# A two-layer graph network: the weighted sum is put inside the second list's branch, and the second FFN's rest is put beside the second attention

## The chip, the cores and the metric

The kernel runs on one core of one Trainium2 chip, in one launch. The metric is the device time of that launch in microseconds. The core has five engines with their own instruction queues, each worked off in order: PE (TensorE, matmuls), DVE (VectorE), ACT (ScalarE), POOL (GpSimd, here the issuer of gathers) and SP (SyncE, the issuer of most other transfers). ACT issues some transfers too. A transfer issued by any of them is carried by the same 16 DMA engines.

## What is computed

`x` is 6250 rows of 256. There are two layers; each is a graph step and then an FFN with a choice of experts, every one on layer-normed rows and added to `x`:

```python
# layer 0, graph: attention over 206250 sorted edges, 4 heads of 64
e = leaky_relu(a_src[src] + a_dst[dst]); p = exp(e - segment_max(e, dst)[dst])
out = relu(segment_sum(p / denom[dst] * h[src], dst) + bias)
# layer 0, FFN: 8 experts, the best 2 of each row, hidden width 1024
out = sum over the 2 of weight * (gelu(ln(x) @ W1[e] + b1[e]) @ W2[e] + b2[e])
# layer 1, graph: a weighted sum over the same 206250 edges
nb = segment_sum(edge_val[:, None] * emb[edge_src], edge_dst)
o = leaky_relu(emb @ W1.T + b1 + (nb + nb * emb) @ W2.T + b2);  out = o / norm(o)
# layer 1, FFN: 4 experts of width 512; the gates come from an attention
# over 131072 other, unsorted edges and a loop at each node (4 heads of 4)
g = gates(gat(x @ W_gat, edge_index)); out = sum_e g_e * (gelu(x @ W1[e]) @ W2[e])
```

## The kernel before

All matrices are float32. The rows of `x` stay in SBUF as `X`, 49 blocks of 128 rows. Edges are taken in tiles of 128, and 8 tiles (`Q`) make a piece. A gather fetches 128 table rows by an index column; POOL issues one for each tile (L1214 in the attentions, L234 in the weighted sum).

The work is staged in time, as the trace shows it:

1. Checks of the first edge list, then the first attention (`gat_stream` with `s0`), to 2245 us.
2. The first FFN (`ffn0`, `routed_ffn`): 56 tiles of 256 sorted rows, 2475 to 3342 us. Each tile has 32 matmuls of L601, four transposes of L586, 32 matmuls of L614. Beside it runs a generator: `sorted_edges` sorts the second edge list (172 steps), then `runs_of` turns the first list into the tables of the weighted sum (indices `si_d`, weights `wab_d`, places `dab_d`), in two chunks of rows. After each FFN tile the code takes four steps, "for _ in range(4): next(beside, None)". A step ends at a `yield`. This part is not ordered by hand: the program order gives priorities to a scheduler, which fills the engines' queues when the kernel is built.
3. The FFN's result is fetched (`yy`, seven loads) and added to `X` (L632).
4. The weighted sum (`fast`, from L1885): `X` is layer-normed (L256) into the table `tab_ef`; then for each piece 8 gathers, the sums of runs on ACT (L1920) and DVE (L1922), one-hot matmuls that place the sums (L2011), and once a block of rows is whole, a chain of functions `side`, `dense`, `norm`, `next_ln`, `next_h`, one link a step. `next_h` writes the row of the second attention's table `tab_1f` (L1986) and the same with one part more into `ha_d` (L1987). When four blocks are done, `start(g)` puts the second FFN's work for them on a list.
5. The second FFN (`dense_ffn`) computes all 4 experts for every row: `inner` is four matmuls (L1654) and a gelu on ACT (L1659), `outer` eight matmuls (L1665), a copy on ACT (L1670) and a write to `y_d` (L1671). A call of `beside()` takes one piece of work off the list. The weighted sum calls it three times per step, and after its last step calls it until the list is empty.
6. A flag, found while sorting, says whether the second list may be taken the fast way: `tc.If(v1 == 1)`. Inside, `layer1_fast` loads `si1s`, `HN`, `dl1s` and `il1s`, prepares the node values and runs `gat_stream` with `s1` (99 pieces). Its own `beside` is called five times per piece and adds the gated results of the FFN, read from `y_d`, to `X` (L1756).

In stages 1, 4, 5 and 6 the order of the main loops is written out by hand ("with tc.manual_schedule()"): each engine gets its instructions in the order of the code. The lines that set the pace of stage 6 are

```python
g = piece[q] = mp.tile([P, Q, W], F32, name="g", bufs=9)      # L1212: freed after messages(q)
...
beside()                                                       # five times in each step
```

Instructions inside a branch are not mixed with instructions outside it. Memory for tiles comes from pools; a pool opened where an earlier one lay waits until the earlier one's tiles are done with.

Of the kernel before, what the change touches and what calls it, by code (L numbers as in the profile page):

```python
# [32 lines left out]
P = 128  # L33
LN_EPS = 1e-5
BIG = float(2**100)
CH = 7
# [35 lines left out]
def tile_kernel(ctx, tc, src_ins, out):  # L72
# [1447 lines left out]
    def runs_of(s, sp, pp, si, wab, dab):  # L1520
# [19 lines left out]
        def turned(dst, src):  # L1540
            d, t = (a.rearrange("p (r j) -> p r j", j=Q) for a in (dst, src))
            for j0 in range(0, Q, 4):
                pt = pp.tile([P, 4, P], F32, name="pt_s")
                for j in range(4):
                    nc.tensor.transpose(pt[:, j], t[:, :, j0 + j], ident)
                nc.scalar.copy(d[:, :, j0:j0 + 4].rearrange("p r j -> p j r"), pt)

        for c in range(-(-npiece // P)):
# [4 lines left out]
            nc.vector.tensor_copy(b, a.bitcast(I32))  # L1553
            nc.vector.tensor_scalar(x, b, 0.0, float(N), op0=OP.is_lt, op1=OP.mult)
            nc.vector.tensor_add(b, b, x)
            nc.vector.tensor_scalar(b, b, 0.0, float(N - 1), op0=OP.max, op1=OP.min)
            yield
            y = room("B1")
            turned(y, b)
# [10 lines left out]
            turned(d, b)  # L1570
            yield
            load(w, I["edge_weight"], c, nr)
            wt = room("A0")
            turned(wt, w)
            yield
            d3 = d.rearrange("p (r j) -> p r j", j=Q)
            first = d3[:, :, 0:1].to_broadcast([P, P, Q])
            for k, op in enumerate((OP.is_equal, OP.not_equal)):
                m = room(("A1", "B1")[k])
                nc.vector.tensor_tensor(m.rearrange("p (r j) -> p r j", j=Q), d3, first, op=op)  # L1580
                nc.vector.tensor_mul(m, m, wt)
# [103 lines left out]
    def layer1_fast(s1, si1, dl1, il1, ha_d, tab_1, y_d):  # L1685
# [3 lines left out]
        with tc.tile_pool(name="g1f", bufs=1) as g1, tc.tile_pool(name="f1w", bufs=2) as fp:  # L1689
            si = g1.tile([P, s1.C * P], I32, name="si1s")  # L1690
            nc.sync.dma_start(si, si1)
            HN = g1.tile([P, NT, W1 + H1], F32, name="HN")
            nc.sync.dma_start(HN, ha_d)
# [75 lines left out]
            def beside():  # L1769
                if work:  # L1770
                    work.pop(0)()
                return bool(work)
# [5 lines left out]
    def fast(flag_s0, last_d, dl_d):  # L1778
# [104 lines left out]
        ha_d = dram.tile([P, NT, D1 + 2 * H1], F32, name="ha_d")  # L1883
        y_d = dram.tile([NT, P, C1, D], F32, name="y_d")
        with tc.tile_pool(name="n1e", bufs=2) as mp:  # L1885
            for t0, n in chunks(NT, CH):
                em = mp.tile([P, CH, D], F32, name="em")
                layernorm(mp, em, X[:, t0:t0 + n, :], n)
                nc.sync.dma_start(tab_e[t0 * P:(t0 + n) * P].rearrange("(t p) d -> p t d", p=P), em[:, :n])
        with tc.tile_pool(name="n1f", bufs=1) as ep, tc.tile_pool(name="n1fw", bufs=2) as mp, \  # L1890
                tc.tile_pool(name="n1f_ps", bufs=1, space=PSUM) as pp, \
                tc.tile_pool(name="f1_ps", bufs=2, space=PSUM) as fpp:
            si = ep.tile([P, npiece * Q], I32, name="si8")
            nc.sync.dma_start(si, si_d)
            wab = ep.tile([P, 2, npiece * Q], F32, name="wab")
            nc.sync.dma_start(wab, wab_d.rearrange("k p t -> p k t"))
            dab = ep.tile([P, npiece * 2], F32, name="dab")
            nc.sync.dma_start(dab, dab_d)
            w12 = ep.tile([P, 2, KD, D], F32, name="w12")
            nc.sync.dma_start(w12[:, 0], I["L1_gnn_W1"].rearrange("(k p) f -> p k f", p=P))  # L1900
            nc.sync.dma_start(w12[:, 1], I["L1_gnn_W2"].rearrange("(k p) f -> p k f", p=P))
            bb = ep.tile([P, 2, D], F32, name="bb12")
            nc.sync.dma_start(bb[:, 0], rows(I["L1_gnn_b1"]))
            nc.sync.dma_start(bb[:, 1], rows(I["L1_gnn_b2"]))
            bias = ep.tile([P, D], F32, name="bias12")
            nc.vector.tensor_add(bias, bb[:, 0], bb[:, 1])
            wg = layer1_weights(ep)
            room, start, beside = dense_ffn(ep, mp, fpp, y_d)
            ips = place_iota(pp)
            acc, piece, runs, ems, sums_of = {}, {}, {}, {}, {}  # L1910

            def sum_runs(q):

                g = piece.pop(q)
                r = [mp.tile([P, D], F32, name=f"run{i}", bufs=3) for i in range(2)]
                for j in range(Q):
                    for i in range(min(2, j + 1)):
                        w = wab[:, i, q * Q + j:q * Q + j + 1]
                        if j == i:
                            nc.scalar.activation(r[i], g[:, j, :], AF.Copy, scale=w)  # L1920
                        else:
                            nc.vector.scalar_tensor_tensor(r[i], g[:, j, :], w, r[i], op0=OP.mult, op1=OP.add)  # L1922
                oh = mp.tile([P, 2, P], F32, name="oh", bufs=3)
                nc.vector.tensor_tensor(oh, ips[:, None, :P].to_broadcast([P, 2, P]),  # L1924
                                        dab[:, 2 * q:2 * q + 2, None].to_broadcast([P, 2, P]), op=OP.is_equal)
                runs[q] = r, oh

            def move(i, kept):

                whole = []  # L1930
                for b in range(NT):
                    of = s0.parts_of(b)
                    if i in of:
                        if b not in sums_of:
                            sums_of[b] = pp.tile([P, D], F32, name="bacc1", bufs=2)
                            ems[b] = mp.tile([P, D], F32, name="emb", bufs=3)
                            nc.sync.dma_start(ems[b], tab_e[b * P:(b + 1) * P])
                        nc.tensor.matmul(sums_of[b], shift_to(s0, i, b), kept, start=(i == of[0]), stop=(i == of[-1]))
                        if i == of[-1]:
                            whole.append(b)  # L1940
                return whole

            def side(b):
                sd = mp.tile([P, D], F32, name="sd_", bufs=2)
                nc.vector.scalar_tensor_tensor(sd, ems[b], 1.0, sums_of.pop(b), op0=OP.add, op1=OP.mult)
                eT = mp.tile([P, KD, P], F32, name="eT")
                transposed(pp, eT, ems.pop(b))
                sT = mp.tile([P, KD, P], F32, name="sT")
                transposed(pp, sT, sd)
                return eT, sT  # L1950

            def dense(b, eT, sT):
                po = pp.tile([P, KD, P], F32, name="pt").rearrange("p k e -> p (k e)")
                for k in range(KD):
                    nc.tensor.matmul(po, eT[:, k], w12[:, 0, k], start=(k == 0), stop=False)
                for k in range(KD):
                    nc.tensor.matmul(po, sT[:, k], w12[:, 1, k], start=False, stop=(k == KD - 1))
                o = mp.tile([P, D], F32, name="on")
                nc.vector.tensor_add(o, po, bias)
                nc.vector.scalar_tensor_tensor(o, o, 0.2, o, op0=OP.mult, op1=OP.max)  # L1960
                return o

            def norm(b, o):
                sq = mp.tile([P, D], F32, name="sq", bufs=1)
                ss = mp.tile([P, 1], F32, name="ss")
                nc.scalar.activation(sq, o, AF.Square, accum_out=ss)
                nc.scalar.activation(ss, ss, AF.Sqrt)
                nc.vector.tensor_scalar_max(ss, ss, 1e-12)
                nc.vector.reciprocal(ss, ss)
                nc.vector.scalar_tensor_tensor(X[:, b, :], o, ss, X[:, b, :], op0=OP.mult, op1=OP.add)  # L1970

            def next_ln(b):
                xl = mp.tile([P, 1, D], F32, name="xl1")
                layernorm(mp, xl, X[:, b:b + 1, :], 1)
                return xl

            def next_h(b, xl):
                o = b % GB * P
                xT = room(b // GB)[:, :, o:o + P]
                transposed(pp, xT, xl[:, 0, :])  # L1980
                ph = pp.tile([P, KD, P], F32, name="pt")[:, 0, :D1 + 2 * H1]
                for k in range(KD):
                    nc.tensor.matmul(ph, xT[:, k], wg[:, k], start=(k == 0), stop=(k == KD - 1))
                h = mp.tile([P, D1 + 2 * H1], F32, name="h1")
                nc.vector.tensor_copy(h, ph)
                nc.sync.dma_start(tab_1[b * P:(b + 1) * P], h[:, :D1 + H1])  # L1986
                nc.sync.dma_start(ha_d[:, b, :], h)  # L1987
                if b % GB == GB - 1 or b == NT - 1:
                    start(b // GB)

            chain = {side: dense, dense: norm, norm: next_ln, next_ln: next_h}


            with tc.manual_schedule():
# [88 lines left out]
```

## Time and profile before

| what | value |
|---|---|
| median of 3 runs | 6830.59 us (6827.94 to 6841.34) |
| the profiled execution | 6821.2 us |
| its span, first to last instruction | 6819.3 us |
| instructions | 61938 |
| busy: PE, DVE, ACT, POOL | 58%, 59%, 17%, 62% of the span |
| granted TensorE clock, mean | 0.746 of full speed |
| moved by DMA | 822.99 MB, mean 121 GB/s |

How to read what follows. A line of the timeline gives start, length, engine, code line, instruction, the tile written and the tiles read, their shapes, how many instructions are merged, and in brackets how long the engine had been idle and what released it. "SPq" and "ACTq" are instructions with which SP and ACT issue a transfer. A line of a table by stage gives the window, its length, then busy time and number of instructions of each engine, the granted TensorE clock, the busy share of the DMA engines and the GB/s. "issue" as a releaser means that nothing in the profile held the engine.

### The profile page before, as it was taken

How to read it: one execution, taken by the hardware profiler on the slowest of the kernel's cores; microseconds unless marked ns; L12 is line 12 of the kernel's file. 1: busy time of each engine (PE TensorE's matmuls, PEld its weight loads, DVE VectorE, ACT ScalarE, POOL GpSimd, SP SyncE). 2: the span in 40 equal slices, each digit the busy share in tenths (PEclk: the TensorE clock that was granted, in tenths of full speed). 3: DMA queues.
4: the chain of work that ended last, by engine and by line, in shares of the span. 5: the costliest groups of instructions: out<-in, count | busy, mean ns of one | idle time of the engine just before them, and what ended most of it. 6: DMA issues, size and time to landing. Idle time of an engine off the chain costs nothing.

```text
span 6819.3 us, 61938 instructions
## 1 busy us (share of the span) xinstructions
PE 3924.9 (58%) x17463; PEld 2934.8 (43%) x17463; DVE 4025.0 (59%) x9984; ACT 1166.6 (17%) x2834; POOL 4252.7 (62%) x4320
## 2 busy tenths in 40 slices
PE   4466665666666579998624566666666665111111
PEld 3344444444444468886513444444444443111111
DVE  5455555555555872443356565555566651788888
ACT  2000000000000112232112233323333332000000
POOL 0777777777777012332167777777777772777774
PEclk9677777777777589998856787778787887555555
DMA  4545555545554145556543444444444441223222
GB/s 135 139 137 139 138 138 139 138 138 138 138 137 128 45 128 194 186 185 206 163 152 105 110 115 113 112 112 113 112 114 114 113 113 53 64 66 66 68 66 56
DMA packets 502756, 822.99 MB, mean 121 GB/s; under 512 B 149744, under 2 KB 321987, under 8 KB 502370
## 3 DMA queue, kind: packets, MB, share of 16 engines
q0 software_dynamic: 190880, 462.26, 25.6%
q1 hardware_dynamic: 298854, 345.00, 16.5%
q10 hardware_dynamic: 12668, 11.68, 0.6%
q8 instruction: 141, 2.31, 0.1%
q14 instruction: 213, 1.74, 0.1%
HBM read 743.88 MB, written 77.89 MB: 121 GB/s over the span
## 4 chain that ended last, share of the span: by engine, by line
PE 26%; DVE 22%; POOL 19%; issue 15%; DMA 13%; ACT 4%; DVEq 0%; SPq 0%; another core or an unknown queue 0%; POOLq 0%; ACTq 0%
POOL g L1214 15%; DVE run L1922 7%; DMA g<-tab,si 7%; PE ph L601 5%; PE py L614 4%; POOL g L234 4%; PE acc L2011 4%; PE acc L1316 3%; PE pf L1654 2%; DMA g<-tab_1f,si1s 2%; DVE X L1756 2%; PE pf L1665 2%; DMA g<-tab_ef,si 2%; DVE g L1293 1%; PE pt L263 1%
## 5 line engine op out<-in xcount | busy, mean ns | idle before, releaser
L234 POOL DMA_INDIRECT g<-tab_ef,si x1616 | 1688.6, 1045 | 591.0 <-issue 437.0
L1214 POOL DMA_INDIRECT g<-tab,si x1612 | 1540.8, 956 | 494.3 <-issue 408.9
L1316 PE MATMUL acc<-g,oh 128*128 128x264 f32 x3224 | 1042.5, 488 | 338.8 <-DVE g L1293 333.9
L1922 DVE SCALAR_TENSOR_TENSOR run<-g,wab,run 128x256 f32<-128x256 f32 x2626 | 1088.8, 478 | 98.9 <-DMA g<-tab_ef,si 65.7
L1316 PEld LDWEIGHTS acc<-g,oh 128*128 128x128 f32 x3224 | 772.0, 247 | 560.4 <-DVE g L1293 394.5
L1214 POOL DMA_INDIRECT g<-tab_1f,si1s x787 | 770.1, 979 | 247.8 <-issue 213.3
L2011 PE MATMUL acc<-run,oh 128*128 128x256 f32 x808 | 336.9, 559 | 857.5 <-DVE oh L1924 857.2
L2011 PEld LDWEIGHTS acc<-run,oh 128*128 128x128 f32 x808 | 195.0, 265 | 993.4 <-DVE oh L1924 834.6
L1246 DVE TENSOR_TENSOR z<-g,nd 128x32 f32<-128x32 f32 (+1 forms) x301 | 57.7, 192 | 752.3 <-DMA g<-tab,si 654.2
L1293 DVE TENSOR_TENSOR g<-g,pe 128x2048 f32<-128x2048 f32 (+2 forms) x301 | 486.8, 1617 | 0.0
L1316 PE MATMUL acc<-s,oh 128*128 128x72 bf16 x1267 | 96.7, 251 | 601.4 <-DVE s L1298 601.4
L1654 PE MATMUL pf<-xt,w 128*128 128x512 f32 (+1 forms) x832 | 424.6, 650 | 1.5 <-ACT h L1659 1.0
L1665 PE MATMUL pf<-w,h 128*128 128x256 f32 x1568 | 413.9, 417 | 12.6 <-ACT h L1659 12.6
L601 PE MATMUL ph<-xe,w 128*128 128x256 f32 x1792 | 404.7, 382 | 0.0
L614 PE MATMUL py<-w,h 128*128 128x256 f32 x1792 | 400.7, 381 | 0.0
L577 POOL DMA_INDIRECT xg<-tab_x,gi x112 | 123.2, 1100 | 408.1 <-PE pt L586 322.4
L1665 PEld LDWEIGHTS pf<-w,h 128*128 128x128 f32 x1568 | 333.7, 214 | 86.8 <-ACT h L1659 17.5
L601 PEld LDWEIGHTS ph<-xe,w 128*128 128x128 f32 x1792 | 341.3, 192 | 45.6
L614 PEld LDWEIGHTS py<-w,h 128*128 128x128 f32 x1792 | 337.2, 191 | 43.3
L1316 PEld LDWEIGHTS <-oh 128*128 128x128 bf16 x1267 | 90.2, 134 | 605.2 <-issue 500.8
L1235 PEld LDWEIGHTS <-ot 128*128 128x128 bf16 x2879 | 116.1, 102 | 457.7 <-DVE ot L1224 403.3
L617 POOL DMA_INDIRECT tab_y<-y,so x112 | 118.6, 1059 | 296.6 <-DVE y L616 292.4
(486 smaller groups left out, 5689.4 us busy)
## 6 DMA issues: line engine op xcount, KB each, us to landing
w<-in_L_ffn_W SPq DMA_DIRECT2D x112, 1024.0 KB
db<-s_d SPq DMA_DIRECT2D x299, 256.0 KB
g<-tab_ef,si POOLq DMA_INDIRECT x1616
g<-tab,si POOLq DMA_INDIRECT x1612
y_d<-y SPq DMA_DIRECT2D x196, 128.0 KB
yb<-y_d SPq DMA_DIRECT2D x49, 512.0 KB
g<-tab_1f,si1s POOLq DMA_INDIRECT x787
yy<-tab_y SPq DMA_DIRECT2D x7, 1792.0 KB
```

Of the source, the lines that this page charges most:

```text
L234: nc.gpsimd.indirect_dma_start(out=dst, out_offset=None, in_=table, in_offset=bass.IndirectOffsetOnAxis(ap=si[:, t:t + 1], axis=0))
L577: nc.gpsimd.indirect_dma_start(out=xg[:, i, :], out_offset=None, in_=tab_x, in_offset=bass.IndirectOffsetOnAxis(ap=gi[:, 2 * j + i:2 * j + ...
L601: nc.tensor.matmul(ph, w1[:, k, f * P:(f + 1) * P], xe[:, k, :], start=(k == 0), stop=(k == KD - 1))
L614: nc.tensor.matmul(py, hs[f][:, i * P:(i + 1) * P], w2[:, f, :], start=(f == 0), stop=(f == FC - 1))
L1214: nc.gpsimd.indirect_dma_start(out=g[:, j, :DH + H], out_offset=None, in_=tab, in_offset=bass.IndirectOffsetOnAxis(ap=si[:, t0 + j:t0 + j ...
L1293: nc.vector.tensor_mul(gh, gh, ps[i][:, o:o + n, :, None].to_broadcast([P, n, H, CD]))
L1316: nc.tensor.matmul(acc[b].rearrange("p s w -> p (s w)"), oh[:, t - a], m_, start=(t == lo), stop=(t == hi))
L1654: nc.tensor.matmul(ph[:, :n], w1[:, e, k, f * P:(f + 1) * P], xts[g][:, k, :n], start=(k == 0), stop=(k == KD - 1))
L1665: nc.tensor.matmul(py[:, :D], hs[g, e, f][:, j * P:(j + 1) * P], w2[:, e, f, :], start=(f == 0), stop=(f == FC - 1))
L1756: nc.vector.scalar_tensor_tensor(X[:, b, :], v[:, e, :], gates[:, j, e:e + 1], X[:, b, :], op0=OP.mult, op1=OP.add)
L1922: nc.vector.scalar_tensor_tensor(r[i], g[:, j, :], w, r[i], op0=OP.mult, op1=OP.add)
L2011: nc.tensor.matmul(acc[i], oh[:, k], r[k], start=(q % 2 == 0 and k == 0), stop=(last and k == 1))
```

## The change

Three things are changed.

- The weighted sum becomes a function, `weighted_sum(room, start, beside, HN)`, with the layer norm that fills `tab_ef` at its head. A new function `with_ffn(then)` opens pools for the second FFN, `HN` and `si1s`, calls `dense_ffn`, the weighted sum and then `then`. The flag is read and the branch entered before all this; the weighted sum is traced once in each arm.
- `next_h` writes its result into `HN` in SBUF, and `tab_1f` from there. `ha_d` is gone. The weighted sum no longer empties the FFN's list at its end. The second attention's `beside` first takes FFN work, and adds gated results only when none is left. In the other arm `finish` empties the list first.
- In `runs_of` a chunk has 17 steps where it had 8: each `turned` yields after each of its two halves, and a few vector operations get a step of their own. `run` has 2 buffers for 3, `kept1` 2 for 3; the FFN's tiles come from a pool of their own (`f1o`).

```diff
 # runs_of
                 nc.scalar.copy(d[:, :, j0:j0 + 4].rearrange("p r j -> p j r"), pt)
+                yield
...
             nc.vector.tensor_copy(b, a.bitcast(I32))
+            yield
             nc.vector.tensor_scalar(x, b, 0.0, float(N), op0=OP.is_lt, op1=OP.mult)
+            yield
             nc.vector.tensor_add(b, b, x)
+            yield
...
-            turned(y, b)
+            yield from turned(y, b)
...
-            turned(d, b)
-            yield
+            yield from turned(d, b)
             load(w, I["edge_weight"], c, nr)
             wt = room("A0")
-            turned(wt, w)
-            yield
+            yield from turned(wt, w)
...
                 nc.vector.tensor_tensor(m.rearrange("p (r j) -> p r j", j=Q), d3, first, op=op)
+                yield
                 nc.vector.tensor_mul(m, m, wt)
 # layer1_fast
-    def layer1_fast(s1, si1, dl1, il1, ha_d, tab_1, y_d):
+    def layer1_fast(s1, si, dl1, il1, HN, tab_1, y_d, rest):
-            si = g1.tile([P, s1.C * P], I32, name="si1s")
-            nc.sync.dma_start(si, si1)
-            HN = g1.tile([P, NT, W1 + H1], F32, name="HN")
-            nc.sync.dma_start(HN, ha_d)
...
             def beside():
-                if work:
+                if not rest() and work:
                     work.pop(0)()
                 return bool(work)
 # fast
-        ha_d = dram.tile([P, NT, D1 + 2 * H1], F32, name="ha_d")
+        def weighted_sum(room, start, beside, HN):
...
-                r = [mp.tile([P, D], F32, name=f"run{i}", bufs=3) for i in range(2)]
+                    r = [mp.tile([P, D], F32, name=f"run{i}", bufs=2) for i in range(2)]
...
-                h = mp.tile([P, D1 + 2 * H1], F32, name="h1")
-                nc.vector.tensor_copy(h, ph)
-                nc.sync.dma_start(tab_1[b * P:(b + 1) * P], h[:, :D1 + H1])
-                nc.sync.dma_start(ha_d[:, b, :], h)
+                    nc.vector.tensor_copy(HN[:, b, :], ph)
+                    nc.sync.dma_start(tab_1[b * P:(b + 1) * P], HN[:, b, :D1 + H1])
...
-                while beside():
-                    pass
+        def with_ffn(then):
+            with tc.tile_pool(name="f1e", bufs=1) as ep, tc.tile_pool(name="f1o", bufs=2) as fp, \
+                    tc.tile_pool(name="f1_ps", bufs=2, space=PSUM) as fpp:
+                HN = ep.tile([P, NT, D1 + 2 * H1], F32, name="HN")
+                si = ep.tile([P, C1s * P], I32, name="si1s")
+                nc.sync.dma_start(si, si1)
+                room, start, beside = dense_ffn(ep, fp, fpp, y_d)
+                weighted_sum(room, start, beside, HN)
+                then(si, HN, beside)
         v1 = nc.values_load(flag1[0:1, 0:1], min_val=0, max_val=1,
                             skip_runtime_bounds_check_because="a comparison: 0 or 1")
         with tc.If(v1 == 1) as cmp1:
-            layer1_fast(s1, si1, dl1, il1, ha_d, tab_1, y_d)
+            with_ffn(lambda si, HN, rest: layer1_fast(s1, si, dl1, il1, HN, tab_1, y_d, rest))
         with cmp1.Else():
+            def finish(si, HN, rest):
+                while rest():
+                    pass
+            with_ffn(finish)
```

## The prediction

> **What bounds the kernel now.** I read first the table of engine busy time by stage, cut where the work changes, because the page's 58% PE, 59% DVE and 62% POOL are means over stages with different limits.
>
> ```profile
> core 0: us, PE busy (x) PEld busy (x) DVE busy (x) ACT busy (x) POOL busy (x), PEclk, DMA share, GB/s
> 3142.00:3228.00 86.00, 58.20 (x257) 48.07 (x257) 28.12 (x38) 23.05 (x36) 13.52 (x16) 0.82 0.52 165
> 3342.00:3442.00 100.00, 0.00 (x0) 0.00 (x0) 77.06 (x254) 3.65 (x9) 0.98 (x1) 0.52 0.64 212
> 3442.00:5630.00 2188.00, 1350.59 (x4160) 897.78 (x4160) 1294.78 (x3354) 617.49 (x1296) 1688.57 (x1616) 0.77 0.41 114
> 5661.00:5730.00 69.00, 61.34 (x265) 45.77 (x265) 0.47 (x2) 20.49 (x48) 0.19 (x1) 0.96 0.20 60
> 5730.00:6741.00 1011.00, 181.95 (x2554) 145.14 (x2555) 818.67 (x2473) 78.23 (x253) 770.10 (x787) 0.50 0.30 68
> ```
>
> Both sums over edges (3442 to 5630, 5730 to 6741) are paced by POOL, which issues one gather after another: 770 us busy of 1011 in the second, and its waits there are nearly all "issue". Between them, 5661 to 5730, only PE works: 61 us of the second FFN. That is the stage the change aims at. The timeline around it says who waits for whom:
>
> ```profile
> 5661.35 0.32 SPq L1986 DMA_DIRECT2D tab_1f<-h  x1
> ...
> 5722.82 0.19 POOL L1137 IOTA s_nid<- 128x49 f32 x1 [99.78 <-PE pf L1665]
> ...
> 5724.14 0.32 SPq L1691 DMA_DIRECT2D si1s<-si  x1
> ...
> 5730.40 0.96 POOL L1214 DMA_INDIRECT g<-tab_1f,si1s  x1 [7.39 <-DMA vec<-in_L_ffn_ln_gamma]
> ```
>
> The table that the second attention gathers from is complete with the write issued at 5661.35. POOL nevertheless stands idle until the last FFN matmul (its node-number tile lies in memory the FFN still holds), then until the index table si1s is loaded.
>
> Next, the passage from the first FFN to the weighted sum, which the branch will now cut:
>
> ```profile
> 3395.31 5.23 DVE L632 SCALAR_TENSOR_TENSOR X<-yy,g,X 128x256 f32<-128x256 f32 x13
> ...
> 3429.70 2.35 DVE L256 TENSOR_SCALAR em<-X,mv,rs 128x256 f32<-128x256 f32 x7
> 3436.28 0.33 SPq L1894 DMA_DIRECT2D si<-si_d  x1
> 3436.39 0.39 ACTq L1625 DMA_DIRECT2D w<-in_L_ffn_W  x1
> ...
> 3449.64 6.55 ACTq L1630 DMA_DIRECT2D bt<-in_L_ffn_b  x1
> ...
> 3456.29 0.91 ACT L1920 ACTIVATE run<-g,wab 128x256 f32<-128x256 f32 x2 [26.86 <-DMA bb<-in_L_gnn_b]
> ```
>
> See that DVE goes from the last X update straight into the layer norm, a quarter of which it did before 3400; and that ACT, after issuing the two weight loads at 3436, is not free until the bias load's issue ends at 3456.2.
>
> Last, PE in the first FFN, where the run lists are made:
>
> ```profile
> 3170.51 7.07 PE L614 MATMUL py<-w,h 128*128 128x256 f32 x32
> 3191.28 1.09 PE L1545 MATMUL pt_s<-ident,A 128*128 128x128 f32 x4 [12.40 <-DVE A L1556]
> ...
> 3218.28 1.09 PE L1545 MATMUL pt_s<-ident,B 128*128 128x128 f32 x4 [9.44 <-DMA B<-in_edge_weight]
> ```
>
> The list's transposes (L1545) stand in PE's queue ahead of the next tile's matmuls and wait for data. The L601 groups of successive tiles begin at 3142.70, 3164.45, 3201.09 and 3227.98: 85.3 us for three tiles. Undisturbed tiles after that are 14.25 us apart, so 42.5 us are lost, 7.5 in the first and 35.0 in the other two.
>
> **1. The FFN's rest leaves the path.** The first gather can follow the table's last write. Issue 5661.35 plus 0.32, some 2 us to land as an estimate (si1s took about 5.9 from issue to gather, index load and wake-up together), puts it near 5664 instead of 5730.40: gain 66 us. si1s and HN are then already in SBUF; the HN load (5.9 us of DVE wait) and 49 ha_d writes of 0.42 us on SP vanish, beside other work, so nothing more. The weighted sum's own tail, 5630 to 5661, keeps its chain and its interleaved FFN steps. Bounds 58 to 67.
>
> **2. What it costs beside the attention.** About 50 steps are left (26 of four L1654 matmuls, 20 of eight L1665, some empty), 61.3 us of PE. The attention calls for work five times per piece of 8 gathers, so they occupy ten pieces. A piece lasts 1011/98.4 = 10.3 us; PE's own work is 182/98.4 = 1.85 us, less in the first seven pieces. At clock 0.96 PE needs 6.1 + 1.85 = 8 us per piece: it fits. Against this speaks the Trainium skill, "TensorE: Matmul & The Clock Gate", "What's actually happening": after an idle window of about 3.4 us the clock falls to half. The row agrees for the attention as it stands, 0.50 throughout. By that rule the rest costs 61.3 × 0.96/0.50 = 118 us, with PE's own 13.6 us per piece, a lag of 33 us after ten pieces; by the row of the drained stage, none. The mean of the weighted sum, which has the same steps interleaved, is 0.77: 76 us, 9.5 per piece. I take that; in the first pieces nothing holds the FFN steps apart, so PE should stay busy. The lag's cover is the nine g buffers: gather s+3 needs piece s-6, freed about four pieces earlier, some 35 us of slack. Behind each FFN matmul group stand pd, zt and the sums on PE; DVE waits for pd, ACT for zt. DVE is 81% busy, so it makes up 2 us per piece in the 85 pieces that follow. Gelu against Exp costs table loads on ACT (1.28 us each by the trace), which is busy 78 of 1011 us. SP gets 20-odd y_d writes among the db loads, which run three pieces ahead. Cost 3 us, bounds 0 and 20.
>
> **3. The branch moves ahead of the layer norm.** DVE can no longer mix the two. X updates are paced by the yy loads (the last starts at 3395.3) and end near 3400.5 either way. Now 31 us of DVE follow; then all 49 tiles: seven chunks at about 5.6 us, 40 us, so 9 more. The branch itself: at the kernel's first one the flag is written at 65.8 and DVE works at 66.84, so 1 us (bounds 0 and 5, since the code is traced twice and longer). Moved with it: w, w and bt are issued on ACT ahead of the layer norm's Sqrt, not behind it; si1s on SP ahead of the em writes takes 0.3 us of a queue idle then. ACT was held 19.8 us (3436.4 to 3456.2) before, with 3.3 MB of list and weight loads beside them; now only si1s (0.5 MB) and yy's end compete, so about 14 us: ACT is free near 3416 where the first Sqrt would be due near 3407; DVE can run only two chunks of statistics ahead. Another 10 us (bounds 0 and 16). What comes back: si's load (5.2 us) no longer shares the DMA engines with 4 MB of weights, 1 us off; and the branch at 5723 goes, in term 1. Sum: 9 + 1 + 10 - 1 = 19, say 20 later (bounds 8 and 28). The first gather moves from 3442.3 to about 3462.
>
> **4. Smaller list steps.** By the code 16 yields become 34. The sort has 172, four are taken per tile, 224 places in 56 tiles: the lists now end in tile 52, not 47, still inside. The loads start as before (as soon as their buffers are free), but the second chunk's transposes rank two to four tiles later, so the in_src data (landed 3186) and s_dst (3199) are there. Of the 35 us, 4 are the transposes' own; the DVE casts that wait for those loads (14.7 and 8.2 us) still stand ahead of the FFN's y and xe on DVE, and PE has about 7 to 12 us in hand: some 9 us remain, and 2 for the weights. 35 - 15 = gain 20. Bounds: 31 if all waits hide, 0 if the order on PE hardly moves.
>
> **5. Two buffers instead of three for run and kept.** The ACT write of run q+2 needs the matmuls of q done. In the trace the matmuls of one piece end at 4410.0 and the ACT write two pieces later starts at 4421.9: 12 us spare. kept is used in the next step. Zero; if PE fell a piece behind, a few us each.
>
> **Sum.** Against the profiled execution's 6821.2 us (span 6819.3): -66 + 3 + 20 - 20 = -63, 6758. The median of the runs shown is 6830.6, 9.4 above that execution; the same difference gives 6767.
>
> **Rivals.**
> - *The front costs little and the lists nearly vanish* (14%): ACT is held for less than the statistics last and all list waits hide: -66 + 9 - 31 + 1, about 6744. For it: no wait in the first chunk; against: the bias issue visibly held ACT.
> - *The list steps change nothing* (12%): transposes keep their place because PE takes them as they become ready: -66 + 3 + 20, 6788.
> - *The attention stalls, slower* (4%): each FFN step makes pd and zt wait, DVE falls behind, g buffers run out. It decides when 50 steps hold up the stage for more than 103 (ten pieces) + 35 (slack) + 66 us, over 4.1 us a step; a cold full step measures 3.4 (L1654, x4). At 5 us a step it loses 250 - 204 = 46 us: 6877. Against: most of the last group's steps are a quarter as wide.
> - *The gathers still wait for the FFN* (4%), through shared memory or a wait on y_d: -20 + 20, 6831. Against: the FFN's tiles get pools of their own that stay open.
> - The forecast as summed: 66%.
>
> A measurement of this kernel tells about 0.2% (13.7 us) from no change. Faster by more: 66 + 14 + 12 = 92%; same 4%; slower 4%. All terms at their good ends give 6740 (-67 + 0 + 8 - 31), at their bad ones 6820 (-58 + 20 + 28 + 0). They are independent: half widths of 4.5, 10, 10 and 15 make about 21 by squares, 6746 to 6788 for the likeliest alone. The range takes in the first two rivals and part of the bad ends: 6735 to 6800.
>
> **What would show it.** Right: the first gather from tab_1f within 5 us of the last tab_1f write; pf matmuls inside the second attention's first 110 us, POOL idle there still "issue"; about 1090 us from its first gather to the end; the first tab_ef gather some 120 us after the first FFN's last matmul instead of 101; three list tiles' loss near 22. Wrong: POOL waiting on DVE s or g in the attention, a first Sqrt that does not wait for bt, or L614 groups still broken by 10 us waits.

## The result and the profile after

The changed kernel takes 6765.36 us (median of 4, 6753.2 to 6777.92), the kernel before 6829.86 (4 runs in all). The ratio is 0.9902, interval 0.9881 to 0.9923: 53 to 81 us less. The profiled execution took 6766.15 us, its span is 6764.4.

The runs below stand in four groups, each with the kernel before beside it, which took 7968 us with e1 to e4, 7875 with e5 to e8, 6823 with e9 and 6808 with e10 to e12; in the two slow groups PE's results reached the other engines late, as lines of e3 will show, so their times and their stages with gathers are compared only within a group.

First the stage table of the changed kernel (the last row is the rest of the second attention without its end):

```profile
core 0: us, PE busy (x) PEld busy (x) DVE busy (x) ACT busy (x) POOL busy (x), PEclk, DMA share, GB/s
3438.00:5634.00 2196.00, 1358.58 (x4137) 897.92 (x4138) 1294.82 (x3343) 617.17 (x1292) 1703.38 (x1616) 0.77 0.39 111
5676.00:5779.00 103.00, 71.94 (x428) 52.71 (x427) 38.30 (x115) 25.59 (x62) 78.16 (x82) 0.81 0.33 73
5779.00:6686.00 907.00, 168.22 (x2358) 134.86 (x2358) 775.85 (x2347) 73.59 (x236) 692.16 (x706) 0.50 0.30 69
```

The stage in which only PE worked is gone; PE's work stands in the attention's first 103 us, and POOL's count there (82 gathers) is that of an undisturbed stage. The same 103 us of the kernel before, for comparison:

```profile
5730.00:5833.00 103.00, 13.31 (x194) 10.27 (x195) 42.25 (x124) 4.40 (x16) 77.31 (x81) 0.50 0.28 63
```

PE has 58.6 us more in it, POOL issues no gather less. The timeline of the changed kernel at the start of the attention:

```profile
5668.27 0.18 POOL L1137 IOTA s_nid<- 128x49 f32 x1 [34.16 <-PE pt L263]
...
5669.58 0.38 SPq L1983 DMA_DIRECT2D tab_1f<-HN  x1
...
5676.14 0.96 POOL L1214 DMA_INDIRECT g<-tab_1f,si1s  x1 [7.69 <-DMA vec<-in_L_ffn_ln_beta]
...
5680.20 9.68 PE L1657 MATMUL pf<-xt,w 128*128 128x512 f32 x16 [4.07 <-ACT y L1673]
```

POOL's node numbers (L1137) are now released by the weighted sum's last transpose, not by the last FFN matmul; the first gather starts 6.6 us after the table's last write is issued, with FFN matmuls still to come. The passage ahead of the weighted sum:

```profile
3382.55 2.18 DVE L632 SCALAR_TENSOR_TENSOR X<-yy,g,X 128x256 f32<-128x256 f32 x5
...
3385.89 9.04 ACTq L1633 DMA_DIRECT2D bt<-in_L_ffn_b  x1
3395.03 1.28 ACT L242 ACT_TABLE_LOAD   x1 [74.71 <-DMA w<-in_L_ffn_W]
...
3396.66 0.39 DVE L244 RECIPROCAL rs<-sd 128x7 f32<-128x7 f32 x2 [5.01 <-ACT sd L242]
...
3438.61 0.99 POOL L234 DMA_INDIRECT g<-tab_ef,si  x1 [110.23 <-issue]
```

The layer norm no longer begins among the X updates, and the bias load holds ACT for 9 us; yet DVE waits for ACT only 5.01 us. Last, PE in the first FFN, while the run lists are made:

```profile
3178.45 7.07 PE L601 MATMUL ph<-xe,w 128*128 128x256 f32 x32
...
3197.74 10.18 PE L601 MATMUL ph<-xe,w 128*128 128x256 f32 x32 [4.88 <-DVE xe L589]
...
3239.75 1.09 PE L1545 MATMUL pt_s<-ident,B 128*128 128x128 f32 x4 [5.59 <-DMA B<-in_edge_weight]
```

Waits of 4.88 and 5.59 us are left where 12.40 and 9.44 stood.

The two profiled spans differ by 54.9 us, made up so (start of the first FFN, its length, and so on to the end):

| stretch | before | after | difference | predicted |
|---|---|---|---|---|
| start to first FFN's first L614 | 2484.3 | 2487.9 | +3.6 | 0 |
| first FFN, first to last L614 | 857.4 | 838.7 | -18.7 | -20 |
| its end to first tab_ef gather | 100.6 | 111.9 | +11.3 | +20 |
| first to last tab_ef gather | 2179.8 | 2194.5 | +14.7 | 0 |
| to first tab_1f gather | 108.3 | 43.0 | -65.3 | -66 |
| second attention to the end | 1088.9 | 1088.3 | -0.6 | +3 |

Two rows need an explanation: the weighted sum's +14.7, and the front's 11 where 20 stood. The +3.6 at the start stays open: e9 to e12 begin at 2486.5 to 2489.8 too, but in the group of e1 to e4 the changed kernels (2833.0 and 2829.2) do not begin later than the old ones (2832.3 and 2832.7). And agreement of a row isn't yet proof of its cause. My theory was that the terms are independent and the 65 us come from running the rest beside the attention; the rivals were that the gathers wait anyway, that the attention stalls, and that the lists change nothing.

### The profile page after: what moved, and what is told of

It reads as the page before. It is cut to its first block, busy times and chain, and to the rows that moved or that the text cites. A ratio compares the mean times of both kernels' runs of the same rounds, so it can differ in the third digit from the quotient of the medians.

```text
span 6764.4 us, 61972 instructions
## 1 busy us (share of the span) xinstructions
PE 3944.6 (58%) x17463; PEld 2945.7 (44%) x17463; DVE 4031.9 (60%) x9984; ACT 1168.1 (17%) x2836; POOL 4269.1 (63%) x4320
## 4 chain that ended last, share of the span: by engine, by line
PE 26%; DVE 22%; POOL 20%; issue 14%; DMA 14%; ACT 4%; DVEq 0%; ACTq 0%; SPq 0%; another core or an unknown queue 0%; POOLq 0%
POOL g L1214 15%; DVE run L1920 7%; DMA g<-tab,si 7%; PE ph L601 5%; PE py L614 5%; POOL g L234 4%; PE acc L2007 4%; PE acc L1316 3%; PE pf L1657 2%; DMA g<-tab_1f,si1s 2%; DMA g<-tab_ef,si 2%; DVE X L1756 2%; PE pt L263 1%; DVE g L1293 1%; DVE oh L1107 1%
## 5 line engine op out<-in xcount | busy, mean ns | idle before, releaser
L1293 DVE TENSOR_TENSOR g<-g,pe 128x2048 f32<-128x2048 f32 (+2 forms) x301 | 487.0, 1618 | 0.0
L1657 PE MATMUL pf<-xt,w 128*128 128x512 f32 (+1 forms) x832 | 443.8, 676 | 11.7 <-ACT y L1673 8.8
L601 PE MATMUL ph<-xe,w 128*128 128x256 f32 x1792 | 407.6, 385 | 4.9 <-DVE xe L589 4.9
L614 PE MATMUL py<-w,h 128*128 128x256 f32 x1792 | 398.6, 380 | 0.0
L601 PEld LDWEIGHTS ph<-xe,w 128*128 128x128 f32 x1792 | 343.4, 194 | 51.3 <-DVE xe L589 5.3
L614 PEld LDWEIGHTS py<-w,h 128*128 128x128 f32 x1792 | 336.8, 191 | 42.8
L1316 PEld LDWEIGHTS <-oh 128*128 128x128 bf16 x1267 | 90.2, 133 | 596.2 <-issue 493.3
L604 ACT ACTIVATE h<-ph,pa 128x256 f32<-128x256 f32 x448 | 211.9, 473 | 443.5 <-PE ph L601 443.3
```

Source lines behind the costliest of these rows:

```text
L601: nc.tensor.matmul(ph, w1[:, k, f * P:(f + 1) * P], xe[:, k, :], start=(k == 0), stop=(k == KD - 1))
L604: nc.scalar.activation(h, ph, AF.Gelu, bias=pa[:, f:f + 1])
L614: nc.tensor.matmul(py, hs[f][:, i * P:(i + 1) * P], w2[:, f, :], start=(f == 0), stop=(f == FC - 1))
L1293: nc.vector.tensor_mul(gh, gh, ps[i][:, o:o + n, :, None].to_broadcast([P, n, H, CD]))
L1316: nc.tensor.matmul(acc[b].rearrange("p s w -> p (s w)"), oh[:, t - a], m_, start=(t == lo), stop=(t == hi))
L1657: nc.tensor.matmul(ph[:, :n], w1[:, e, k, f * P:(f + 1) * P], xts[g][:, k, :n], start=(k == 0), stop=(k == KD - 1))
```

## The experiments

**e1 and e10: the rest of the FFN is not spread.** The changed kernel, but the list is emptied ahead of the attention:

```diff
-            with_ffn(lambda si, HN, rest: layer1_fast(s1, si, dl1, il1, HN, tab_1, y_d, rest))
+            def first_finish(si, HN, rest):
+                while rest():
+                    pass
+                layer1_fast(s1, si, dl1, il1, HN, tab_1, y_d, rest)
+            with_ffn(first_finish)
```

> The changed kernel, but the fast arm empties the second FFN's list between the weighted sum and the second attention, as before. Theory (the rest of the FFN beside the attention is what takes about 65 us off the path): the gap from the last tab_ef gather to the first tab_1f gather goes from 42.9 us back towards 108 minus the two loads and the second branch (si1s and HN are already there, so the node-number tile is the only thing behind the last matmul): about 100; the attention itself stays at about 1088; time about 6822 against 6765, that is 0.998 to 1.000 of the kernel before. Rival (the first gather waits for something else, such as the branch or the table's write): the gap stays near 43 and the time near 6765.

Measured: the gap from the last tab_ef gather to the first tab_1f gather is 82.8 us, against 142.7 and 143.3 in e4 and e3 of the same group, which have the old tail, and 81.1 in e2, which spreads the FFN; ratio to the kernel before 0.9977 (0.9958 to 0.9996). So about 60 us of the gap stay away though the FFN is not spread: my account of the tail falls. The same edit in the fast group, e10:

> The changed kernel with the FFN's list emptied between the weighted sum and the second attention, asked again on a chip on which the kernel before takes about 6830 us. On the other chip its first tab_1f gather was not held (gap 82.8 us, as without emptying): POOL waits for memory of the FFN's pools, not for the FFN. Theory now: what took 65 us off is that the attention's tiles no longer lie where the FFN's lay; the order of the FFN's steps decides only where PE's lag goes. PE starts the first piece's work about 60 us late instead of spreading it, the nine buffers of g cover about 35, so the attention takes 15 to 30 us more (1103 to 1118) and the time is 6780 to 6795. Rival A (the emptied list holds POOL here as it held it before): gap about 100, time 6822. Rival B (the buffers cover all of it): gap 43, attention 1088 to 1092, time 6765.

Gap 46.4, attention 1088.4, median 6735.57 where the kernel before takes 6808.18: ratio 0.9887 (0.9871 to 0.9904). Rival B holds: emptying the list costs nothing that these intervals show. The timeline of e10:

```profile
5659.52 0.19 POOL L1137 IOTA s_nid<- 128x49 f32 x1 [37.05 <-PE pt L263]
...
5660.82 0.38 SPq L1983 DMA_DIRECT2D tab_1f<-HN  x1
...
5667.90 0.96 POOL L1214 DMA_INDIRECT g<-tab_1f,si1s  x1 [8.20 <-DMA il1s<-il]
...
5698.94 7.07 PE L1668 MATMUL pf<-w,h 128*128 128x256 f32 x32
...
5706.30 0.18 PE L1235 MATMUL pd<-NB,ot 128*128 128x24 bf16 x1
```

POOL gathers from 5667.90 while PE works off the FFN; the attention's first matmul (pd) comes 38.4 us after the first gather instead of 6.1 in the kernel before. Of those 32 us 10 are left at the first product of gathered rows (L1293), which comes 68.9 us after the first gather where it comes at 59.1 in the kernel before; and POOL doesn't notice these, as the next runs show. What the change must do is let POOL start; in which order PE does the rest doesn't matter here.

What lets it start is either that the attention's tiles no longer lie where the FFN's lay, or that there is no branch between. These moved together, and no run parts them, but the trace of the kernel before shows what each did. The instructions that take its branch, L2035 (after "to" stands the branch at the arm's end):

```profile
L2035 POOLq COMPARE_BRANCH  x2: 34/38/41, 5613.9 to 6732.3; - x2
...
L2035 SPq COMPARE_BRANCH  x2: 38/38/39, 5723.7 to 6814.1; - x2
```

Each engine took the branch when its own queue had come to it. POOL was inside at 5613.9, 109 us before it could write its node numbers at 5722.82: the branch did not hold it, the memory did. SP came to the branch only at 5723.7, behind the FFN's last write to `y_d` (5723.04), and issued the load of si1s after it. So two things held the first gather until then: POOL's memory, and SP's queue, which could not take the load across the branch. The change removes both: si1s is issued at 3384.81, and without a branch between, il1s goes out in e10 at 5663.00, between two `y_d` writes.

**e7, e8, e11, e12: how much PE work the attention hides.** From the end of the weighted sum on, each matmul group of the FFN is computed n times into the same sums:

```diff
-            for k in range(KD):
-                nc.tensor.matmul(ph[:, :n], ...)
+            for _ in times:
+                for k in range(KD):
+                    nc.tensor.matmul(ph[:, :n], ...)
...
                 weighted_sum(room, start, beside, HN)
+                times[:] = range(2)   # or 3; the same around the py matmuls
```

> The changed kernel in which every matmul group of the FFN's rest that runs beside the second attention is computed twice into the same sums; the result is the same. 58 us more of PE in the attention's first 103 us. Theory (nine g buffers give about 35 us of slack, and DVE makes up what lag is left): PE needs about 130 us for what 103 held, a lag of 27 us that the buffers cover; the stage stays at 1088 to 1095 us, time 6765 to 6772. Rival (the attention stalls with each FFN step, since pd and zt stand behind it): the stage grows by about the added 58 us, 1140 and more, time 6820.

> As the one with the groups computed twice, but three times: about 117 us more of PE. Theory: ten pieces need about 188 us of PE instead of 103, a lag of 85 us, of which the buffers cover about 35: POOL waits for g there for the first time, and the stage grows by 45 to 60 us, time about 6815. If the slack were far larger (work waits in POOL's lead and DVE catches up): growth under 15 us. If there were none: growth of 85 us or more.

In this slow group gather 81 starts 154 us after the first with one copy (e6), 182 with two and 221 with three; the attention took 1520.8, 1565.7 and 1606.4 us, and the ratios to the kernel before were 1.0015 (1.0001 to 1.003) and 1.0054 (1.0025 to 1.0083). Against the one copy of e6 the stage grows by 45 and 86 us: the copies are paid as if there were no slack. The same edits in the fast group:

> Each matmul group of the FFN's rest computed twice beside the attention, on a chip on which the kernel before takes about 6830 us. In the changed kernel PE is busy 72 of the first 103 us, some 58 of them with the FFN. Theory: PE needs 130 us for the first ten pieces, a lag of 27 us or less, inside the 35 us of the g buffers: attention 1088 to 1095, time 6765 to 6772. On the other chip the first 80 gathers took 182 us instead of 154, but there the stage has no slack at all, since gathers land late. Rival (each step holds pd and zt and the stage stalls with it): attention 1115 to 1145.

> Each matmul group of the FFN's rest computed three times beside the attention, on a chip on which the kernel before takes about 6830 us. Theory (growth = lag less 35 us of slack): PE needs about 188 us for the first ten pieces, lag 85, attention 45 to 55 us longer than 1088, time about 6815; POOL waits for g there. Rival (slack is much larger): growth under 15 us. Rival (no slack): 85 us or more.

Attention 1093.0 us with two copies, 1139.3 with three, against 1088.4 with one: +4.6 and +50.9. Medians 6742.04 and 6787.19; ratios to the kernel before 0.9896 (0.9879 to 0.9912) and 0.9964 (0.995 to 0.9978). The theory of a slack holds. Its size can be read from the timelines, two copies first, then three:

```profile
5757.48 0.28 DVE L1293 TENSOR_TENSOR g<-g,pe 128x128 f32<-128x128 f32 x1
...
5760.16 0.94 POOL L1214 DMA_INDIRECT g<-tab_1f,si1s  x1 [7.73 <-ACT y L1676]
```

```profile
5788.38 0.28 DVE L1293 TENSOR_TENSOR g<-g,pe 128x128 f32<-128x128 f32 x1
...
5791.07 0.94 POOL L1214 DMA_INDIRECT g<-tab_1f,si1s  x1 [50.70 <-issue]
```

The gather shown is number 73, the first that needs a g buffer back, and it follows the first L1293 by 2.7 us. That L1293 comes 95.1 us after the first gather with two copies and 137.7 with three; POOL's waits, less the usual 0.3, are 7.4 and 50.4. Both say that the wait begins when L1293 is later than 87.5 us. In the kernel before it comes at 59.1: the slack is 28 us, where I had 35. With one copy it comes at 61.3, so the rest of the FFN as it is uses 2 us of it. The stage table of the run with three copies:

```profile
5650.00:5753.00 103.00, 103.00 (x382) 68.80 (x381) 3.46 (x13) 10.28 (x20) 68.03 (x72) 1.00 0.21 39
```

PE is full, at full clock, and POOL stops after its 72 gathers.

**e2, e3, e4: lists and buffers.** e2 is the changed kernel with the old `runs_of`; e3 is the kernel before with the new one; e4 is the kernel before with

```diff
-                r = [mp.tile([P, D], F32, name=f"run{i}", bufs=3) for i in range(2)]
+                r = [mp.tile([P, D], F32, name=f"run{i}", bufs=2) for i in range(2)]
...
-                            kept = mp.tile([P, D], F32, name="kept1", bufs=3)
+                            kept = mp.tile([P, D], F32, name="kept1", bufs=2)
```

> The changed kernel with the 16 coarse list steps of before. Theory (the smaller steps are worth the 18.6 us by which the first FFN got shorter): first FFN from its first L614 to its last back at 857 us, PE waits of about 12 and 9 us on the list's transposes are there again, everything after it unchanged; time 6784 against 6765. Rival (the first FFN got shorter for another reason, for instance the scheduler's new priorities because less work follows it outside a branch): the first FFN stays near 838 and the time near 6765.

> The kernel before with only the smaller list steps. Theory: first FFN 838 instead of 857 us; weighted sum, its passage from the FFN (first tab_ef gather 101 us after the last FFN matmul) and its end as before; time 6811 against 6830 (ratio 0.9973). Rival (the gain belongs to the branch being put ahead, or is given back at once by the layer norm, which waits for the yy loads): 6826 to 6830.

> The kernel before with two buffers instead of three for run and for kept1, nothing else. Two readings of the 14.8 us by which the weighted sum got longer. A: the two buffers bring the DVE bursts into another phase against the gathers, so more gathers are stretched: about 40 gathers of 2 us and more instead of 20, the gather region 2190 to 2195 instead of 2180 us, time 6840 to 6845. B: it has nothing to do with the buffers (chance from run to run, or the memory addresses): the region stays at 2180, or moves in runs with three buffers as much as in runs with two; time 6830 within 0.2%.

The first FFN takes 855.8 us in e2 and 857.5 in e4 (coarse steps), 838.9 in e3 (small steps). Over all profiles it is 855.8 to 857.5 in three with coarse steps and 838.3 to 842.0 in eleven with small ones: the steps are worth 14 to 19 us, whatever else is in the kernel. The times say less: ratios 1.0004 (0.999 to 1.0018) in e2, 0.9996 (0.9981 to 1.0011) in e3, 1.0013 (0.9999 to 1.0026) in e4. For e3, 0.9973 was expected; its interval doesn't hold it, so in that group the FFN's gain doesn't show in the time; the gather stages scatter by more (the weighted sum takes 2506.5 us in e4, 2532.9 in e3).

e2's ratio was missed by more. Its gap is 81.1 us, 62 less than e3's, but its attention takes 1559.7 us against 1518.1 and 1511.4 in e3 and e4. Most of the tail's gain is given back, and e1's attention (1557.0) says the same without spreading. Gather 73 of e3, then of e2:

```profile
6554.12 0.28 DVE L1293 TENSOR_TENSOR g<-g,pe 128x128 f32<-128x128 f32 x1
6556.82 1.04 POOL L1214 DMA_INDIRECT g<-tab_1f,si1s  x1 [17.93 <-issue]
```

```profile
6559.26 0.28 DVE L1293 TENSOR_TENSOR g<-g,pe 128x128 f32<-128x128 f32 x1
6561.96 0.94 POOL L1214 DMA_INDIRECT g<-tab_1f,si1s  x1 [54.91 <-ACT y L1670]
```

In e3, with nothing of the FFN left, the first L1293 is already 106.1 us after the first gather (6448.06). Late rows are not the reason, whatever e11's expectation says of late gathers: the attention's first three pieces get theirs 12.4, 22.4 and 32.6 us after the first gather, in the kernel before 12.5, 22.4 and 32.6. PE's results are late:

```profile
6480.69 0.19 DVE L1246 TENSOR_TENSOR z<-g,nd 128x32 f32<-128x32 f32 x1 [4.18 <-DMA g<-tab_1f,si1s]
6481.79 0.71 PE L1235 MATMUL pd<-NB,ot 128*128 128x24 bf16 x13 [9.44 <-DVE z L1247]
...
6506.33 0.36 DVE L1244 TENSOR_REDUCE nd<-pd 128x64 f32<-128x192 f32 x1 [24.30 <-issue]
6506.73 0.19 DVE L1246 TENSOR_TENSOR z<-g,nd 128x32 f32<-128x32 f32 x1
```

The third piece waits for its rows (z). For the fourth the pd matmuls are recorded at 6481.79, but DVE's nd, which reads them, runs 24.5 us later, and the z behind it finds its rows there. In the kernel before nd follows pd's last matmul within about a microsecond. Over the whole span DVE is idle 36 us before its nd instructions there, and 961 to 1094 us in e1 to e8. Why PE's results are late in these groups is open. So the slack is gone before the FFN takes any, and all that PE brings along in e2 (142.0 us after 6417.28) is paid: the rival "the attention stalls" decides when the slack is used up otherwise, a case that the prediction leaves out.

For the buffers: gathers of 2 us and more number 17 in e4 and 14 in e3; and the gather region is the shorter one in e4. Two buffers aren't the longer case. (The changed kernel with three buffers each was not run.)

**The weighted sum's +14.7: chance.** Five profiles of the fast groups have the changed kernel's weighted sum with two buffers (the changed kernel, e9 to e12): 2194.5, 2184.5, 2181.0, 2175.3, 2167.9 us, mean 2180.6, where the kernel before has 2179.8. The rows of the gathers in the pages of the changed kernel and e12, in this order (busy, mean ns, idle before):

```profile
L234 POOL DMA_INDIRECT g<-tab_ef,si x1616 | 1703.5, 1054 | 602.2 <-issue 552.3
```

```profile
L234 POOL DMA_INDIRECT g<-tab_ef,si x1616 | 1676.9, 1038 | 602.5 <-issue 544.3
```

The idle time is the same; the difference is all in how long the gathers take. A long one, in the changed kernel:

```profile
4396.83 5.36 DVE L1920 SCALAR_TENSOR_TENSOR run<-g,wab,run 128x256 f32<-128x256 f32 x13
...
4398.62 1.22 POOL L234 DMA_INDIRECT g<-tab_ef,si  x1 [0.30 <-issue]
4400.14 2.87 POOL L234 DMA_INDIRECT g<-tab_ef,si  x1 [0.30 <-issue]
4402.10 0.42 DVE L1922 TENSOR_TENSOR oh<-ips,dab 128x256 f32<-128x256 f32 x1
```

It begins in DVE's burst of 13 sums and ends 0.5 us after the burst's oh; an ordinary one takes 0.95. The changed kernel's profile has 40 of 2 us and more, the other four 8 to 15, before has 19. How gathers and bursts fall against each other differs from run to run of the same code; what sets it is open.

**e5, e6, e9: the front.** e5 moves the layer norm back ahead of the branch, e6 leaves it inside and puts only the code of the FFN's loads behind it:

```diff
 # e5: this block of weighted_sum stands ahead of v1 = nc.values_load(...); e6: ahead of dense_ffn(...)
+        with tc.tile_pool(name="n1e", bufs=2) as mp:
+            for t0, n in chunks(NT, CH):
...
```

> The changed kernel with the layer norm that fills tab_ef moved back ahead of the branch; the FFN's weight loads stay inside it, now behind the layer norm. Theory (the branch ahead of the layer norm costs the 11.3 us, by keeping DVE from mixing the two and by holding ACT 10 us with the bias issue): layer norm mixed with the X updates again, the first tab_ef gather 98 to 103 us after the first FFN's last matmul instead of 111.9, then as the changed kernel; time 6755 against 6765. Rival (the gain is given back: the loads of si8, the weights and si1s now all start after the branch and hold the first gather): 108 to 112 us and 6765.

> The changed kernel with the FFN's three loads issued on ACT behind the layer norm instead of ahead of it; the branch still stands ahead of the layer norm. It parts the two halves of the front's cost. Theory: ACT held by the bias issue is worth up to 10 us at the first Sqrt, of which DVE's two chunks of statistics cover some: first tab_ef gather 104 to 107 us after the FFN's last matmul instead of 111.9, so 5 to 8 us of the 11.3 belong to the issue and the rest to the lost mixing. Rival (the whole cost is the lost mixing): 111 to 112. Other rival (the bias issue moves in front of the first run on ACT and costs the same there): the first gather comes earlier, but the whole time stays at 6765.

From the FFN's last matmul to the first tab_ef gather: 104.5 us in e5, 109.7 in e6, 112.0 and 112.1 in e7 and e8 of the same group, which have the changed kernel's front. (Times: ratio 0.9977, 0.9954 to 1.0, and 0.9959, 0.9942 to 0.9976.) Both lie between what was expected and the rival. e6 does not part the halves cleanly. This code is ordered by the scheduler, which put the first weight load at the layer norm's start all the same (3710.75) and the bias load into it:

```profile
3717.39 3.54 ACTq L1633 DMA_DIRECT2D bt<-in_L_ffn_b  x1
...
3729.02 2.35 DVE L256 TENSOR_SCALAR em<-X,mv,rs 128x256 f32<-128x256 f32 x7 [2.89 <-DMA tab_ef<-em]
```

DVE's wait of 5 us for ACT is gone, but it now waits 2.89 us for a write of the table. So e6's 2.4 us are a net figure. In e5 the last em is written 90.2 us after the FFN's last matmul, as in the kernel before (90.3), where the changed kernel has 101.8: the layer norm's share of the front is won back in full. Yet e5 doesn't reach 100.6. Its timeline:

```profile
3736.53 2.35 DVE L256 TENSOR_SCALAR em<-X,mv,rs 128x256 f32<-128x256 f32 x7
...
3743.21 0.33 SPq L2027 DMA_DIRECT2D si1s<-si  x1
3743.45 0.40 ACTq L1628 DMA_DIRECT2D w<-in_L_ffn_W  x1
3743.59 0.42 SPq L1888 DMA_DIRECT2D si<-si_d  x1
...
3753.15 1.00 POOL L234 DMA_INDIRECT g<-tab_ef,si  x1 [102.76 <-DMA si<-si_d]
```

14.3 us lie between the last em and the first gather, 10.3 in the kernel before. The branch is hardly to blame: si's load is issued 4.7 us after the last em, before 4.2. But from its issue to the gather, which waits for it, it takes 9.6 us, before 6.0: si1s and the first weights are now issued just ahead of it. So e9 also takes that load out of the way:

```diff
+        ip = keep.enter_context(tc.tile_pool(name="si8p", bufs=1))
+        si8 = ip.tile([P, npiece * Q], I32, name="si8")
+        nc.sync.dma_start(si8, si_d)
         # then the layer norm, then the branch
```

> The changed kernel with the layer norm ahead of the branch, as in the run that moved it, and with the weighted sum's index table si8 loaded ahead of the layer norm into a tile of its own. In the changed kernel si8 is issued 4.2 us after the last em is written, because its tile lies where em lay, and the first gather follows 6.0 us later. Theory (front: mixing 7.5 us, and the si8 load another 6 to 10): first tab_ef gather 92 to 98 us after the FFN's last matmul instead of 111.9, everything else as in the changed kernel; on a chip that takes 6830 us for the kernel before, 6748 to 6755. Rival (the first gather waits for the landing of the last tab_ef write or for the branch anyway): 103 to 105, and 6757.

96.0 us, 15.9 less than in the changed kernel: within the expected 92 to 98, and below the 100.6 of before. Median 6745.6 us where the kernel before takes 6822.63: ratio 0.9887 (0.987 to 0.9903).

```profile
3416.13 2.35 DVE L256 TENSOR_SCALAR em<-X,mv,rs 128x256 f32<-128x256 f32 x7
...
3424.07 0.99 POOL L234 DMA_INDIRECT g<-tab_ef,si  x1 [94.27 <-issue]
```

5.6 us from the last em to the first gather, branch included. The stage is 16 us shorter; that the whole kernel beats the changed one isn't shown, as the two ratios' intervals overlap and they come from different groups.

## Why the prediction was right

- **The FFN's rest leaves the path (-66): -65.3.** Size right, reason half right. The waits I named were the ones that went; but spreading the rest (term 2's working) is not what removes them, since e10 has them gone without it. The prediction also left out that SP's queue, stopped at the branch, held the load of si1s back as well. The table's write to the first gather took 6.6 us, not 5: POOL also waits for il1s and the small vectors.
- **Cost beside the attention (+3): -0.6.** The clock was 0.81 in the 103 us, near the 0.77 I took and not the 0.50 of the rule I weighed. The first group after an idle of 4.07 us did run slowly (9.68 us for 16 matmuls, 7.13 in e10 after 0.48 us), in the sense of the rule of the Trainium skill's "TensorE: Matmul & The Clock Gate", "What's actually happening"; but denser work held the clock up, to 1.00 with three copies. The 0.81 is a mixture: from 5686 to 5716, with PE busy 29 of 30 us, the clock was 1.00, from 5761 to 5779, with 4 of 18, it was 0.50. The slack is 28 us, not 35, and only 2 were used.
- **The branch ahead of the layer norm (+20): +11.3.** This is the step that failed in size, and the term in it is "another 10" for ACT held by the bias issue. ACT was held 10.1 us from 3384.81, not 14, and DVE, which had statistics to do meanwhile, waited 5.01 us once and then wrote two chunks at a stroke. The rest, from the timelines of before and after: from the last X update to the last em DVE works 38.7 us instead of 30.7, so 8.0 for the lost mixing where 9 stood; the X updates end 1.5 us sooner after the last matmul, where no difference was expected; the branch leaves DVE idle for 0.08 us, where 1 stood; from the last em to the gather it is 0.2 less, where 1 less stood. 5.0 + 8.0 - 1.5 - 0.2 = 11.3.
- **Smaller list steps (-20): -18.7,** 14 to 19 over all profiles. Six tiles from 3143.98 to 3255.67 lose 26 us against 14.25 each; I had 22 left of 42.5. (That total was right, its split was not: in the kernel before the second and third tile begin at 3161.41 and 3177.41, where their first L601 matmuls stand, not at 3164.45 and 3201.09.) The 4.88 us wait for xe is the one that the prediction left standing.
- **Two buffers (0): 0** within the scatter, as e4 and e9 to e12 show; the 14.7 us beside it were scatter.
- **The sum (-63): the time fell by 64.5.** Without scatter the terms give -65.3 - 0.6 + 11.3 - 18.7 = -73; the interval, -53 to -81, holds both. That -63 came so near is in part luck: the front was 9 too dear, and the scatter hid it.
- **Rivals.** That the gathers wait anyway is excluded by the timeline, that the lists change nothing by the FFN's length. "The attention stalls" is true where PE's results are late: there about 44 of the tail's 60 us came back in the attention.

## What to carry to other kernels

When an engine waits at a stage's border, ask whether it waits for the other engine's work, only for its memory, or for a load that another queue holds back: with memory of its own, the follower's buffers may hide the work even if it isn't spread. Reckon such a slack as a date, the first instruction that needs a buffer back, and put the delay of the first release against it; it is spent by whatever comes late. A profile's stage can differ by 15 us between runs of the same code: before explaining such a row, look at other profiles that have the code unchanged.

## What was not expected of the hardware

A gather issued by POOL took 2.87 us instead of 0.95 when it fell into 5.4 us of DVE sums back to back. In the changed kernel's weighted sum 430 of the 1616 gathers take more than 1 us, and every one of them overlaps such sums; of the 588 that overlap none, none takes more than 0.99. The Trainium skill's "SBUF — State Buffer", "SBUF: two separate sides", says that GpSimd and DVE share one pair of SBUF ports as an exclusive lock, held for a whole instruction, and that a DVE instruction with two SBUF inputs takes part in it against a GpSimd instruction that reads SBUF. The rows fit in part: one sum lasts 0.41 us, so one lock doesn't explain 1.9 us more, and no run here took the bursts away.

The clock followed the density of PE's work in the same stage: 0.50 with 13 us of it in 103, 0.81 with 72, 1.00 with 103. And in the two slow groups nearly the same instructions took 15 to 17% longer in all, with every engine's busy time the same within 1% (e4 against before) and PE's results late.
